# Layer 0 attention: row maxima taken apart into steps and laid between projections and between exponentials

## The chip, the cores and the metric

The kernel runs on one core of one Trainium2 chip, as one launch. The metric is the device time in microseconds. Five engines work side by side, each through its own queue in order: TensorE (PE, matrix products and transposes, with its weight loads shown as PEld), VectorE (DVE), ScalarE (ACT), GpSimd (POOL) and SyncE (SP, which issues most DMAs).

## The reference, cut to what matters

The program is a network of four layers on x of 2 x 1024 x 1024 (batch, tokens, features), float32, each layer an attention-like part and a feed-forward part, each followed by x + f(x) and a normalization over the features. The change lies in the first part of layer 0:

```
qk = (x @ Wqk_w.T + Wqk_b).reshape(b, n, H, E, 2)      # H = 8 heads, E = 16
q, k = the two last indices of qk;  v = x @ Wv_w.T + Wv_b
scores = einsum('bhqd,bhkd->bhqk', q, k)
attn = softmax(scores, axis=-1) / sqrt(128)
out = einsum('bhsl,bhlv->bhsv', attn, v)
return out @ Wo_w.T + Wo_b
```

So q, k and v have 128 features together (8 heads of 16), and each of the 1024 queries of a batch attends to all 1024 keys in each head.

## The kernel before, in words

Batch after batch goes through all layers (net_kernel). x lies in SBUF as eight tiles of 128 tokens x 1024 features, and a transposed copy xT as eight blocks of 128 features x 1024 tokens. to_xT(tt) (L113 to L123) makes xT of one tile: eight transposes on TensorE (L119) into two PSUM banks, and one eviction each, by VectorE and ScalarE in turn (evac, L94). PSUM is one pool of eight banks of 128 x 512 float32; every ps() takes one, and it is free again when its last reader is done.

For batch 0 x is loaded at the start. For batch 1 its tiles are loaded at the end of the last layer of batch 0, each after the output tile in the same place has been stored (load_x). Then all eight tiles are transposed, and l0(b) begins.

l0 loads wqkv (three tiles: q, k, v), wo, the row l0_bo, up and down through SP, and adds the row to all eight tiles of x on POOL (add_row, L126, one 128 x 1024 addition each). It then works in halves th of 512 tokens:

- Projections (L241 to L259): for each half and each s of q, k, v, eight matmuls of 128 x 128 by 128 x 512 into one bank (mm, L104), then an eviction with bias on VectorE (st, L248). For q and k, eight DMAs on SP (L252) spread the heads: qT[g][th] and kT[g][th] hold four heads each (g = 0, 1), one head in each 32 partitions: 16 features, and more rows which POOL had set to 0 in qT and to 1 in kT. For v, four transposes (L256) and two copies on VectorE (L259).
- maxima(th) (L261): for each of 16 steps (g, 128 queries, half of the keys), four matmuls with 32 rows each (L270), one head each, give scores in four banks, and VectorE reduces each to its row maximum (L281). TensorE is kept one step ahead: the next step's scores are issued after the second reduction. After both halves of the keys, a small reduction writes the negated maximum into nmax (L285). After all queries of a g, nmax is transposed (L291) and added to qT (L292), into the row that meets the ones of kT. So the scores that attend computes have the maximum taken off already.
- attend(th, extra) (L294): for each of 16 steps (g, 128 keys), four score matmuls in the other orientation, keys in partitions (L304), four exponentials on ScalarE from PSUM into pt (L312), and four output matmuls, each into 32 partitions of the bank po (L322). A column of ones in v gives the sums of the exponentials. Step n issues the exponentials of n + 1, the scores of n + 2, the outputs of n, and then what extra has for n. done(g) (from L329) turns the result back with four transposes (L332) and divides by the sums.

The order at the end of l0 (from L464) is written out by hand, inside manual_schedule: maxima(0), attend(0), maxima(1), attend(1). What stands outside of such a block, as projections, memsets and loads did, is ordered by a planner, which may put a later part's loads and memsets between; so the row l1_bv of the next part (L91) and the mask (L502), which need a buffer that add_row or a projection frees, stand among the DMAs and memsets of layer 0. Into attend(1) go, as extra, the output projection of the first half (project), the normalization and the transposes of the result. The feed-forward part follows.

The rows l0_bo, l1_projb and l1_bv share two buffers; weight tiles (w) share eight. All eight are taken by wqkv, wo, up and down; the first weights of the next part (l1_conv) and the mask come into those of wqkv when these are no longer read.

Of the kernel before, what the change touches and what calls it, by code (L numbers as in the profile page):

```python
# [11 lines left out]
AF = mybir.ActivationFunctionType  # L12
# [5 lines left out]
P = 128  # L18
# [3 lines left out]
NT = S // P  # L22
KD = D // P
HALF = 512
# [3 lines left out]
class Net:  # L28
# [174 lines left out]
    def l0(self, b):  # L203
        nc, i = self.nc, self.i
        wqkv = [self.w(i["l0_wqkv"][j]) for j in range(3)]
        wo = self.w(i["l0_wo"])
        row = self.row("l0_bo")
        for tt in range(NT):
            self.add_row(row, tt)
        up = [self.w(i["l0_up"][j]) for j in range(2)]  # L210
        down = [self.w(i["l0_down"][j]) for j in range(2)]
        xd, yd = [[self.dp.tile([D, HALF], F, name=self.nm(n)) for _ in range(2)] for n in ("xd", "yd")]
        with self.tc.tile_pool(name=self.nm("l0a"), bufs=1) as lp, self.tc.tile_pool(name=self.nm("l0b"), bufs=2) as tp:
            bias = self.param(lp, "l0_bqkv", [P, 3])
            idx = self.param(lp, "l0_perm", [P, KD], I)

            def piece(name):
                return lp.tile([P, HALF], F, tag="t", bufs=24, name=self.nm(name))
# [6 lines left out]
            qT, kT = [[[piece(n) for _ in range(2)] for _ in range(2)] for n in ("qT", "kT")]  # L225

            v = [piece("v").rearrange("p (a h e) -> p a h e", a=2, h=8) for _ in range(4)]
            ao = lp.tile([P, NT, P], F, name=self.nm("ao"))
            for g in range(2):
                for th in range(2):  # L230
                    nc.gpsimd.memset(qT[g][th], 0.0)
                    nc.gpsimd.memset(kT[g][th], 1.0)
            for t in v:
                nc.gpsimd.memset(t, 0.0)
                nc.gpsimd.memset(t[:, :, :, 16:17], 1.0)
# [2 lines left out]
            for t in nmax:  # L238
                nc.gpsimd.memset(t, 0.0)

            for th in range(2):  # L241
                for s, dst in ((0, qT), (1, kT), (2, v)):
                    p = self.ps()
                    self.mm(
                        p, [(wqkv[s][:, k * P : (k + 1) * P], self.xcols(k, th * HALF, HALF)) for k in range(KD)]
                    )
                    st = piece("st")
                    nc.vector.tensor_scalar(st, p, bias[:, s : s + 1], None, ALU.add)  # L248
                    if s < 2:
                        for h in range(8):  # L250
                            j = h % 4
                            nc.sync.dma_start(dst[h // 4][th][32 * j : 32 * j + 16, :], st[16 * h : 16 * h + 16, :])  # L252
                        continue
                    p = self.ps()
                    for q in range(4):
                        nc.tensor.transpose(p[:, q * P : (q + 1) * P], st[:, q * P : (q + 1) * P], self.ident)  # L256
                    pv = p.rearrange("p (q h e) -> p q h e", q=4, e=16)
                    for a in range(2):
                        nc.vector.tensor_copy(v[2 * th + a][:, :, :, 0:16], pv[:, 2 * a : 2 * a + 2])  # L259

            def maxima(th):  # L261

                steps = [(g, qt, kh) for g in range(2) for qt in range(4) for kh in range(2)]

                def scores(g, qt, kh):

                    pss = [self.ps() for _ in range(4)]
                    for j in range(4):
                        r = slice(32 * j, 32 * j + 32)
                        nc.tensor.matmul(  # L270
                            pss[j], qT[g][th][r, qt * P : (qt + 1) * P], kT[g][kh][r, :], start=True, stop=True
                        )
                    return pss

                todo = scores(*steps[0])
                for n, (g, qt, kh) in enumerate(steps):
                    pss = todo
                    if kh == 0:
                        mx = self.small([P, 4, 2], "l0mx")
                    for j in range(4):  # L280
                        nc.vector.tensor_reduce(mx[:, j, kh : kh + 1], pss[j], AX.X, ALU.max)  # L281
                        if j == 1 and n + 1 < len(steps):
                            todo = scores(*steps[n + 1])
                    if kh:
                        nc.vector.tensor_reduce(  # L285
                            nmax[g][:, qt].rearrange("p (j e) -> p j e", e=32)[:, :, 16], mx, AX.X, ALU.max, negate=True
                        )
                    if qt == 3 and kh:
                        p = self.ps()
                        for q in range(4):  # L290
                            nc.tensor.transpose(p[:, q * P : (q + 1) * P], nmax[g][:, q], self.ident)  # L291
                        nc.vector.tensor_tensor(qT[g][th], qT[g][th], p, ALU.add)  # L292

            def attend(th, extra):  # L294

# [67 lines left out]
            def project(tt):  # L363
                p = self.ps()
                nc.tensor.transpose(p[:, :P], ao[:, tt, :], self.ident)
                aoT = tp.tile([P, P], F, tag="aoT", name=self.nm("aoT"))
                nc.vector.tensor_copy(aoT, p[:, :P])
                for nh in range(2):
                    p = self.ps()
                    nc.tensor.matmul(p, aoT, wo[:, nh * HALF : (nh + 1) * HALF], start=True, stop=True)  # L370
                    self.add_x(tt, nh, p)
                self.ln_stats(tt)

            def store(th):
                for k in range(KD):
                    nc.sync.dma_start(xd[th][k * P : (k + 1) * P, :], self.xcols(k, th * HALF, HALF))
# [3 lines left out]
            def gather(th, n=KD):  # L380
                for j in range(len(ts[th]), len(ts[th]) + n):
                    t = piece("t")
                    nc.gpsimd.indirect_dma_start(
                        out=t, out_offset=None, in_=xd[th][:],
                        in_offset=bass.IndirectOffsetOnAxis(ap=idx[:, j : j + 1], axis=0),
                    )
                    ts[th].append(t)
# [55 lines left out]
            def back(th):  # L443
                ys = [piece("y") for _ in range(KD)]
                for k, t in enumerate(ys):
                    nc.sync.dma_start(t, yd[th][k * P : (k + 1) * P, :])
                return ys

            def line(th, first, n):


                t4 = [4 * th + q for q in range(4)]
                e = {}
                for tt, m in zip(t4, n[:4]):
                    e.setdefault(m, []).append(lambda tt=tt: first(tt))
                e.setdefault(n[4], []).append(lambda: self.ln_roots(t4))
                for tt, m in zip(t4, n[5:]):
                    e.setdefault(m, []).append(lambda tt=tt: (self.ln_scale(tt), self.to_xT(tt)))
                return e

            def at(extra, n, f):
                extra.setdefault(n, []).append(f)

            got = {}  # L464
            with self.tc.manual_schedule():
                self.table()
                maxima(0)
                attend(0, {})
                maxima(1)
                e = line(0, project, (0, 1, 3, 4, 5, 6, 7, 8, 9))  # L470
                at(e, 9, lambda: store(0))
                at(e, 9, lambda: gather(0))
                attend(1, e)
                project(4)
                project(5)
                e = line(1, project, (-1, -1, 0, 0, 1, 1, 2, 2, 3))
                del e[-1]
                at(e, 3, lambda: store(1))
                for n in (5, 6):
                    at(e, n, lambda: gather(1, 2))  # L480
                at(e, 7, lambda: gather(1, 4))
                blocks(0, e)
                ys = back(0)
                e = line(0, lambda tt: self.add_y(tt, ys), (2, 3, 3, 4, 5, 6, 6, 7, 7))
                blocks(1, e)
# [1279 lines left out]
def net_kernel(tc, ins, out):  # L1765
    with ExitStack() as ctx:
        net = Net(ctx, tc, ins, out)
        for tt in range(NT):
            net.load_x(0, tt)
        for b in range(B):  # L1770
            for tt in range(NT):
                net.to_xT(tt)
            with tc.tile_pool(name=net.nm("l1o"), bufs=1) as op:
                w = net.l1_ffn(b, *net.l1_attn(b, net.l0(b), op))
            net.late(b, net.l2_attn(b, w))
# [100 lines left out]
```

## Time and profile before

| what | us |
|---|---|
| median of 3 runs | 5486.4 |
| these runs | 5469.3 to 5487.4 |
| the profiled execution | 5484.1 |
| its span, first to last instruction | 5482.4 |
| TensorE busy in the span | 5094.7 (93%) |
| VectorE busy | 3189.5 (58%) |
| POOL busy | 2025.3 (37%) |
| ScalarE busy | 1934.7 (35%) |

The mean granted TensorE clock is 0.952 of full speed. In the profile a row such as "61.32 19.24 PE L270 MATMUL ps<-kT,qT 32*128 32x512 f32 x64 [0.40 <-DMA kT<-st]" gives start, length, engine, line, operation, output and inputs, tile in the array, how many instructions are drawn together, and in brackets how long the engine had been idle before and what ended that. One float32 matmul of the program is two matmul rows. The ends of matmuls are modelled, so long rows of TensorE may hold waiting. The stages of layer 0 in batch 0 are: transposes to 15 us, projections from 15.3 to 59.8, maxima(0) to 102.8, attend(0) to 140.9, maxima(1) to 183.7; in batch 1: transposes from 2736.6, projections from 2756.6 to 2803.0, maxima(0) to 2846.0, attend(0) to 2883.8, maxima(1) to 2926.6.

### The profile page before, as it was taken

How to read it: one execution, taken by the hardware profiler on the slowest of the kernel's cores; microseconds unless marked ns; L12 is line 12 of the kernel's file. 1: busy time of each engine (PE TensorE's matmuls, PEld its weight loads, DVE VectorE, ACT ScalarE, POOL GpSimd, SP SyncE). 2: the span in 40 equal slices, each digit the busy share in tenths (PEclk: the TensorE clock that was granted, in tenths of full speed). 3: DMA queues.
4: the chain of work that ended last, by engine and by line, in shares of the span. 5: the costliest groups of instructions: out<-in, count | busy, mean ns of one | idle time of the engine just before them, and what ended most of it. 6: DMA issues, size and time to landing. Idle time of an engine off the chain costs nothing.

```text
span 5482.4 us, 52348 instructions
## 1 busy us (share of the span) xinstructions
PE 5094.7 (93%) x17864; PEld 2576.6 (47%) x17864; DVE 3189.5 (58%) x4380; ACT 1934.7 (35%) x3913; POOL 2025.3 (37%) x1195
## 2 busy tenths in 40 slices
PE   9879988999999999998988899889999999999989
PEld 4346745444444444453444476554444444444533
DVE  3553255269989995324345412542799899953143
ACT  2321232267766541011023312323677665410110
POOL 1013120077778883101010120200777788821010
PEclk8889999999999999999987999999999999999999
DMA  2145211277787995110211432112877979950100
GB/s 89 37 144 180 97 54 36 95 219 212 208 246 223 270 256 178 43 65 8 83 33 33 140 115 93 49 44 98 230 213 204 245 220 262 257 173 36 62 8 31
DMA packets 263134, 725.30 MB, mean 132 GB/s; under 512 B 37424, under 2 KB 54448, under 8 KB 262868
## 3 DMA queue, kind: packets, MB, share of 16 engines
q1 hardware_dynamic: 256596, 700.97, 42.8%
q0 software_dynamic: 6272, 20.98, 1.1%
q8 instruction: 143, 2.34, 0.2%
q14 instruction: 123, 1.01, 0.1%
HBM read 616.70 MB, written 103.02 MB: 131 GB/s over the span
## 4 chain that ended last, share of the span: by engine, by line
PE 52%; DVE 10%; ACT 2%; DMA 1%; issue 1%; POOL 0%; SPq 0%; DVEq 0%; ACTq 0%; POOLq 0%
PE ps L104 22%; PE ps L1191 4%; PE ps L1516 4%; PE ps L1301 4%; DVE h L1198 3%; PE ps L1340 3%; PE ps L1220 3%; PE ps L567 3%; PE ps L119 2%; DVE h L1209 2%; DVE x L175 1%; PE ps L1254 1%; ACT ps L1193 1%; DVE st L152 1%; PE ps L270 1%
## 5 line engine op out<-in xcount | busy, mean ns | idle before, releaser
L1183 POOL TENSOR_TENSOR h<-h,br 128x1024 f32<-128x1024 f32 x512 | 1204.2, 2374 | 24.4 <-DMA h<-dxd 13.3
L1193 ACT ACTIVATE ps<-ps,l_Alog 128x512 f32<-128x512 f32 x1024 | 669.1, 660 | 687.4 <-PE ps L1191 680.6
L1191 PE MATMUL ps<-hi,rep 128*128 128x512 f32 x1024 | 757.5, 740 | 21.0 <-DVE h L1198 14.9
L1198 DVE TENSOR_TENSOR_SCAN h<-ps,h 128x512 f32<-128x512 f32 x512 | 606.3, 1212 | 159.1 <-ACT ps L1193 102.6
L1198 DVE TENSOR_TENSOR_SCAN h<-ps,hst,h 128x512 f32<-128x512 f32 x512 | 642.1, 1298 | 14.5 <-ACT ps L1193 14.3
L1209 DVE TENSOR_TENSOR h<-h,ps 128x1024 f32<-128x1024 f32 x512 | 619.5, 1211 | 0.0
L104 PE MATMUL ps<-w,xT 128*128 128x512 f32 (+1 forms) x1280 | 518.3, 562 | 0.0
L1301 PE MATMUL ps<-xT,w 128*128 128x512 f32 x1024 | 513.7, 605 | 0.0
L1220 PE MATMUL ps<-h,sel 128*32 128x512 f32 x2048 | 409.4, 616 | 73.7 <-DVE h L1209 73.4
L1502 POOL TENSOR_TENSOR x<-x,row 128x1024 f32<-128x1024 f32 x48 | 112.9, 2352 | 883.6 <-PE ps L119 883.6
L141 DVE TENSOR_TENSOR x<-x,ps 128x512 f32<-128x512 f32 x192 | 129.3, 686 | 528.4 <-PE ps L104 377.6
L104 PE MATMUL ps<-xT,w 128*128 128x512 f32 x960 | 421.2, 595 | 0.2 <-DMA w<-l_wqkv 0.2
L1191 PE MATMUL ps<-lo,rep 128*128 128x512 f32 x1024 | 408.6, 399 | 0.0
L104 PEld LDWEIGHTS ps<-w,xT 128*128 128x128 f32 x1280 | 247.3, 195 | 255.5 <-issue 248.5
L1191 PEld LDWEIGHTS ps<-hi,rep 128*128 128x128 f32 x1024 | 195.4, 191 | 346.2 <-issue 239.4
L119 PE MATMUL ps<-ident,x 128*128 128x128 f32 x1024 | 162.8, 314 | 151.9 <-DVE x L175 134.6
L104 PEld LDWEIGHTS ps<-xT,w 128*128 128x128 f32 x960 | 182.1, 190 | 230.1 <-issue 227.7
L1191 PEld LDWEIGHTS ps<-lo,rep 128*128 128x128 f32 x1024 | 195.9, 191 | 200.6 <-issue 195.4
L1149 POOL TENSOR_TENSOR e<-e,one 128x512 f32<-128x512 f32 x64 | 81.5, 1273 | 557.9 <-ACT one L1146 364.4
L166 ACT ACTIVATE rs<-mv 128x1 f32<-128x1 f32 (+2 forms) x88 | 17.9, 203 | 760.1 <-DVE mv L160 759.9
L1301 PEld LDWEIGHTS ps<-xT,w 128*128 128x128 f32 x1024 | 188.3, 191 | 174.3 <-issue 149.7
L1340 PE MATMUL ps<-w,w 128*128 128x512 f32 x512 | 269.0, 607 | 0.0
(272 smaller groups left out, 7628.0 us busy)
## 6 DMA issues: line engine op xcount, KB each, us to landing
h<-dxd SPq DMA_DIRECT2D x512, 512.0 KB
w<-l_in SPq DMA_DIRECT2D x128, 512.0 KB
w<-l_out SPq DMA_DIRECT2D x96, 512.0 KB
w<-l_conv SPq DMA_DIRECT2D x54, 512.0 KB
w<-cvd SPq DMA_DIRECT2D x36, 512.0 KB
w<-l_fw SPq DMA_DIRECT2D x32, 512.0 KB
xcd<-xo SPq DMA_DIRECT2D x64, 256.0 KB
szd<-zo SPq DMA_DIRECT2D x64, 256.0 KB
```

What stands on the lines that cost most here:

```text
L104: self.nc.tensor.matmul(out, lhsT, rhs, start=j == 0, stop=j == n - 1)
L119: nc.tensor.transpose(p[:, j * P : (j + 1) * P], self.x[:, tt, k * P : (k + 1) * P], self.ident)
L567: nc.tensor.matmul(w["p", j // 2][:, 256 * (j % 2) : 256 * (j % 2) + 256], w["w"][j][:, k * P : (k + 1) * P], moving(th, j, k), start=k == ...
L1183: nc.gpsimd.tensor_tensor(hs[k], hs[k], norms[of(k)[0]][1].unsqueeze(1).to_broadcast([P, 2, HALF]), ALU.mult)
L1191: nc.tensor.matmul(dA[k, m], rep[:, 8 * jj + 4 * m + q, :], hl[u, c][n], start=n == 0, stop=n == 1)
L1193: nc.scalar.activation(dA[k, m], dA[k, m], AF.Exp, scale=A[:, g : g + 1])
L1198: nc.vector.tensor_tensor_scan(hs[k][:, m, :], dA.pop((k, m)), hs[k][:, m, :], hst[:, g : g + 1] if u else 0.0, ALU.mult, ALU.add)
L1209: nc.vector.tensor_tensor(hs[k], hs[k], norms[of(k)[0]][3].unsqueeze(1).to_broadcast([P, 2, HALF]), ALU.mult)
L1220: nc.tensor.matmul(py[u, c][32 * j : 32 * j + 32, :], self.sel[:, q, :], hs[k - 1 + j // 2][:, j % 2, :], start=False, stop=q == 3,)
L1301: nc.tensor.matmul(p, w["w"][:, k * P : (k + 1) * P], self.xcols(k, u * HALF, HALF), start=k == 0, stop=k == KD - 1)
L1340: nc.tensor.matmul(p, y[:, cc, t * P : (t + 1) * P], wt[:, cc * HALF : (cc + 1) * HALF], start=c2 == 0 and cc == 0, stop=last,)
L1516: nc.tensor.matmul(acc[tt], y[:, cc * HALF + tt * P : cc * HALF + (tt + 1) * P], w[:, cc * HALF : (cc + 1) * HALF], start=c == 0, stop=c = ...
```

## The change

Three things are done.

1. The projections become a generator qkv(s, th, scalar), which issues two of its eight matmul blocks and then hands back control. With scalar set, the eviction is on ScalarE in place of VectorE. The copies of v are always on ScalarE. They all stand inside the block ordered by hand. First come k and q of half 0, whole. Then the transposes of tiles 4 to 7, which net_kernel no longer does. Then k of half 1. The rest, q of half 1 and v of both halves, makes 14 pieces (4, 5 and 5), one of which follows each step of maxima(0).
2. maxima hands back control after each step too. maxima(1) is no stage of its own any more: one of its 16 steps follows each of the 16 steps of attend(0).
3. add_row for tiles 0 to 3 stands between the memsets of qT and kT and those of v; for tiles 4 to 7 it comes after maxima(0).

```diff
-        for tt in range(NT):
-            self.add_row(row, tt)
...
+            for tt in range(4):
+                self.add_row(row, tt)
             for t in v:
...
-            for th in range(2):
-                for s, dst in ((0, qT), (1, kT), (2, v)):
-                    p = self.ps()
-                    self.mm(
-                        p, [(wqkv[s][:, k * P : (k + 1) * P], self.xcols(k, th * HALF, HALF)) for k in range(KD)]
+            def qkv(s, th, scalar):
+                p = self.ps()
+                for k in range(KD):
+                    nc.tensor.matmul(
+                        p, wqkv[s][:, k * P : (k + 1) * P], self.xcols(k, th * HALF, HALF), start=k == 0, stop=k == KD - 1
                     )
-                    st = piece("st")
+                    if k % 2 and k < KD - 1:
+                        yield
+                st = piece("st")
+                if scalar:
+                    nc.scalar.activation(st, p, AF.Identity, bias=bias[:, s : s + 1])
+                else:
                     nc.vector.tensor_scalar(st, p, bias[:, s : s + 1], None, ALU.add)
+                if s < 2:
+                    dst = (qT, kT)[s]
+                    for h in range(8):
+                        j = h % 4
+                        nc.sync.dma_start(dst[h // 4][th][32 * j : 32 * j + 16, :], st[16 * h : 16 * h + 16, :])
+                    yield
+                    return
+                yield
+                p = self.ps()
+                for q in range(4):
+                    nc.tensor.transpose(p[:, q * P : (q + 1) * P], st[:, q * P : (q + 1) * P], self.ident)
+                pv = p.rearrange("p (q h e) -> p q h e", q=4, e=16)
+                for a in range(2):
+                    nc.scalar.copy(v[2 * th + a][:, :, :, 0:16], pv[:, 2 * a : 2 * a + 2])
+                yield
...
                         nc.vector.tensor_tensor(qT[g][th], qT[g][th], p, ALU.add)
+                    yield
...
                 self.table()
-                maxima(0)
-                attend(0, {})
-                maxima(1)
+                for s in (1, 0):
+                    for _ in qkv(s, 0, False):
+                        pass
+                for tt in range(4, NT):
+                    self.to_xT(tt)
+                for _ in qkv(1, 1, False):
+                    pass
+                side = [f for s, th in ((0, 1), (2, 0), (2, 1)) for f in [qkv(s, th, True)] for _ in range(5 if s else 4)]
+                for n, _ in enumerate(maxima(0)):
+                    for f in side[:1]:
+                        next(f)
+                        del side[0]
+                for f in side:
+                    next(f)
+                for tt in range(4, NT):
+                    self.add_row(row, tt)
+                m = maxima(1)
+                attend(0, {n: [lambda: next(m)] for n in range(16)})
                 e = line(0, project, (0, 1, 3, 4, 5, 6, 7, 8, 9))
...
         for b in range(B):
-            for tt in range(NT):
+            for tt in range(4):
                 net.to_xT(tt)
```

More of the change, by code (lines that the diff above doesn't have):

```diff
@@ L239, in l0 @@
                 nc.gpsimd.memset(t, 0.0)
-            for th in range(2):
-                for s, dst in ((0, qT), (1, kT), (2, v)):
-                    p = self.ps()
-                    self.mm(
-                        p, [(wqkv[s][:, k * P : (k + 1) * P], self.xcols(k, th * HALF, HALF)) for k in range(KD)]
-                    )
-                    st = piece("st")
-                    nc.vector.tensor_scalar(st, p, bias[:, s : s + 1], None, ALU.add)
[L249 to L259, printed above, removed]
+            def qkv(s, th, scalar):
[3 more added lines that the diff above has]
+                        p, wqkv[s][:, k * P : (k + 1) * P], self.xcols(k, th * HALF, HALF), start=k == 0, stop=k == KD - 1
+                    )
+                    if k % 2 and k < KD - 1:
[4 more added lines that the diff above has]
+                else:
+                    nc.vector.tensor_scalar(st, p, bias[:, s : s + 1], None, ALU.add)
+                if s < 2:
[13 more added lines that the diff above has]
+                yield
```

## The prediction, made before the changed kernel was run

> **What bounds the kernel now.** I read the page first (chain of waits, slices), then the busy times in windows cut at the stages of layer 0, then the timeline of single engines inside them. The page's chain is carried by TensorE and little else:
>
> ```profile
> PE 52%; DVE 10%; ACT 2%; DMA 1%; issue 1%; POOL 0%; SPq 0%; DVEq 0%; ACTq 0%; POOLq 0%
> ```
>
> Busy shares over the whole span say little about this change: it touches about 170 us of the first half (15 to 184 us, batch 0) and 190 us of the second (2737 to 2927 us, batch 1). The windows of batch 0 decide there; columns are PE, PEld, DVE, ACT, POOL busy, then granted clock, DMA share, GB/s:
>
> ```profile
> 15.00:37.00 22.00, 20.97 (x50) 8.98 (x48) 2.67 (x4) 0.59 (x1) 16.51 (x8) 1.00 0.53 205
> 37.00:60.00 23.00, 22.04 (x60) 10.00 (x64) 3.05 (x6) 0.00 (x0) 2.47 (x3) 1.00 0.33 82
> 60.00:104.00 44.00, 41.33 (x144) 27.53 (x144) 41.75 (x76) 0.00 (x0) 0.00 (x0) 0.59 0.06 18
> 104.00:141.00 37.00, 36.22 (x268) 10.14 (x264) 2.40 (x6) 32.83 (x64) 0.00 (x0) 0.94 0.00 1
> 141.00:184.00 43.00, 40.73 (x140) 25.52 (x144) 41.46 (x77) 0.00 (x0) 0.00 (x0) 0.64 0.00 0
> ```
>
> Each stage has another master. Projections (15 to 60): TensorE alone. maxima(0) and maxima(1) (60 to 104, 141 to 184): VectorE, 41.5 of 43 us, eight reductions in 4.88 us. TensorE is shown busy too, but its rows are long because they wait for PSUM banks and run at 0.59 of the clock. attend(0) (104 to 141): ScalarE, 2.06 us for four exponentials. So stages with different masters stand in a row, and the change lays them beside each other. Batch 1 adds a hole: its last transposes wait for tile 7 of x, behind which all projections stand.
>
> ```profile
> 2736.64 6.28 PE L119 MATMUL ps<-ident,x 128*128 128x128 f32 x56
> 2754.86 1.94 PE L119 MATMUL ps<-ident,x 128*128 128x128 f32 x8 [11.95 <-DMA x<-x]
> 2756.59 22.79 PE L104 MATMUL ps<-xT,w 128*128 128x512 f32 x48
> ```
>
> **Front part, batch 0.** One projection is 16 matmul rows of 0.43 us, 6.86 us. The first wqkv tile landed at 15.1 us; DMA runs at about 415 GB/s there, so the second one, with which k now starts, lands 1.3 us later: start 16.4. k and q of half 0: 13.7, to 30.1. Transposes of tiles 4 to 7: 4 x 1.06 = 4.2 plus 0.7 for the last eviction, to 35.0. k of half 1: 6.9, to 41.9. Before 42 nothing else is late: l_bqkv landed at 27.3, and 16 DMAs of kT and qT at 0.62 us each on SP end near 38, landing 1.9 us later. Then comes a new wait. Scores of step 1 need kT of half 1, which the DMAs bring:
>
> ```profile
> 57.30 4.94 SPq L252 DMA_DIRECT2D kT<-st  x8
> 61.32 19.24 PE L270 MATMUL ps<-kT,qT 32*128 32x512 f32 x64 [0.40 <-DMA kT<-st]
> ```
>
> The fourth DMA is issued 1.9 us after the first and lands 1.9 us later; with the eviction (0.75) and signals, step 1 begins 5.4 us after k ends, at 47.3. Behind that matmul all side projections are queued on TensorE, so only step 0's reductions are covered.
>
> From there maxima(0) has 15 steps. A step's four scores take 1.07 us at full clock, a side piece of two k-blocks 4 x 0.43 = 1.72. So 12 of the 14 pieces make a step of about 2.85 us, above VectorE's 2.49; the other two (four transposes, 0.66) leave it at VectorE's 2.5. 15 x 1.12 + 12 x 1.76 + 2 x 0.8 = 39.5 on TensorE, 2 for the transposes of nmax in the middle, 4.5 for the last reductions, transposes and addition (before: 99.2 to 103.6): 46, to 93.3. The projection holds one bank, so a step's fourth score waits for the first reduction of the step before (0.75 us after its scores), which ends within the side piece: no cost. The three evictions and four copies given to ScalarE, 0.6 us each, are free: it is idle from 16 to 105 us; without that cover they would cost 4 us. An Identity needs no table load (none stands at L573 or L661). On POOL, add_row(0..3) now stands ahead of the memsets of v and nmax: row l_bo lands at 20.5, so these end near 33, and nmax is first written after 50. Moved add_row(4..7), 9.3 us from about 35, has nobody waiting until project(4); beside such adds a small VectorE operation took 1.80 us in place of 0.16 (2741.24), which here falls into the wait for kT.
>
> Here a rule speaks against the change. The Trainium skill, "TensorE: Matmul & The Clock Gate", Part 1, says that an idle window of about 3.4 us puts the array to half clock and a busy one brings it back. The 4 us idle time before step 1 (k's last matmul and one score group aside) is such a window. The trace agrees on the size: after the 11.95 us hole the clock was 0.50 until about 2761, and the first matmuls took 0.86 in place of 0.43 us. By the rule 3.4 us at half clock cost 1.7; if the gate misses the gap, 0. I take 1.5: attend(0) starts at 94.8, against 102.8: **8.0 us won**.
>
> **Front part, batch 1.** Transposes of tiles 0 to 3: 2736.6 to 2741.3. Weights are there (DMA is busy to 2742.7 with all eight, wqkv first). k, q: to 2755.0, which covers the wait for tile 7; it landed at 2754.8, and hardly later now, since only half of POOL's add_row still runs beside VectorE's last normalization. Transposes: to 2760.0; k of half 1: 2766.9; wait 5.4; 46 + 1.5: 2819.8, against 2846.0: **26.2 us won**, 12 of it the hole and about 3 the half clock behind it.
>
> **attend(0) with maxima(1).** Before: 102.8 to 183.7 and 2846.0 to 2926.6, 80.9 and 80.6 us. Now each of 16 iterations has three matmul groups: scores for attend (1.07), outputs (1.00), scores for maxima (1.07), which follow each other so at full clock:
>
> ```profile
> 112.91 1.06 PE L322 MATMUL ps<-pt,v 128*32 128x512 f32 x8
> 113.91 1.14 PE L304 MATMUL ps<-qT,kT 32*128 32x512 f32 x8
> 114.98 1.06 PE L322 MATMUL ps<-pt,v 128*32 128x512 f32 x8
> ```
>
> The same skill's "TensorEngine Tiling (Array Packing)", Key Properties, says that a change of the tiling mode drains TensorE. Here groups of 32 rows and 32 columns alternate and a group still takes 1.0 to 1.07, where two matmuls of 0.43 in a row need 0.86: the drain is within 0.2 us. So its price is in my groups already; counted again it would be 0.4 an iteration, 6 us a stage.
>
> The lower bound is thus 3.14 us. But PSUM has eight banks: one for the outputs, four with scores for maxima, four for attend. One is missing, so the fourth score matmul of attend waits for the first reduction of the scores just made. Nothing in the trace has both streams; the nearest row has attend with transposes that take two banks:
>
> ```profile
> 214.44 1.09 PE L119 MATMUL ps<-ident,x 128*128 128x128 f32 x8
> 215.47 2.37 PE L304 MATMUL ps<-qT,kT 32*128 32x512 f32 x8
> 217.76 1.07 PE L322 MATMUL ps<-pt,v 128*32 128x512 f32 x8
> ```
>
> There the score group took 2.37, half of it waiting for a bank, and the iteration 4.32. With a reduction (0.68) as releaser in place of a copy and an exponential (1.1), I get 1.07 + 0.75 + 1.0 + 1.0 = 3.85. Below 3.14 nothing can go; the upper end is 5, if two reductions must be waited for. Sum: 14 x 3.85 = 53.9; two last iterations without scores of attend 5; first groups 3.2; in the middle and at the end all reductions must end before nmax is transposed, 3.3 and 4; done(1) 1.5; half clock at its start 2: **72.9 us, 8 won per batch**. attend(1) and all behind it are unchanged and start earlier, TensorE being the chain; l_conv loads still come long before their use.
>
> **Sum.** 8.0 + 26.2 + 2 x 8 = 50 us. The profiled run took 5484.1 (span 5482.4), so 5434; the median of the three runs is 2.3 higher: 5436, 0.9% faster. About 0.5% (27 us) is what a measurement of this kernel can tell from no change; its three runs spread over 18 us.
>
> **Rivals.**
> (1) Waits for banks or SP eat more. If an iteration takes 4.8, each stage is 13 longer and 24 remain: 5462. The same comes from SP: row l_bv (L91) waits for the last add_row; before, it stood ahead of the q DMAs (issued 39.00, then 39.42). If it still does, kT comes up to 11 us later per batch: 5458. Against: add_row(4..7) now follows the transposes, so it should be queued after kT and qT of half 0.
> (2) The clock stays at half in the merged stage, and the kernel gets slower. For: maxima had TensorE "busy" and yet 0.50 for 30 us. A score group cold takes 2.0 (three in 6.06 from 102.79); an iteration 3 x 1.9 + 0.75 = 6.5; the stage about 114, 33 longer than now. 66 lost against 34 won in front: 5518. It decides above 5.6 us per iteration. Against: in maxima the array moves data for 0.86 of 2.49 us (35%), here 2.58 of 3.85 (67%); in 262 to 269 us PE was busy 2.1 of 3.4 (62%) and kept 1.00, and attend(0) woke it within 5 us.
> (3) It goes better: reductions never hold a bank back (3.3 per iteration), no half clock: 16 + 7 more, 5413.
> (4) It doesn't do what it says: the order stays stage by stage (the side pieces all wait at the end of the queue) and only the hole is filled: about 5472, or, with lost overlap elsewhere, no change.
>
> **Chances.** As worked 0.50 (5421 to 5451), rival 1 0.20, rival 2 0.09, rival 3 0.11, rival 4 0.10. The range 5408 to 5474 takes in the first, second and fourth of these cases. Faster by over 0.5% (below 5459): 0.50 + 0.11 + half of rival 1, 0.71. Slower by over 0.5%: most of rival 2, 0.08. Between: 0.21.
>
> **What would show it.** Right: no idle PE row of 12 us at 2743; kT's DMA named before the second score group with about 4 us; steps of 2.9 us in maxima(0) at clock 1.00; iterations of 3.7 to 4 in attend(0), its scores released by VectorE. attend(1) starts near 168 and 2877 (2893 less batch 0's 16). Wrong: granted clock 0.5 through the merged stage, iterations above 5, or SP standing at row l_bv with kT behind it.

## The result, and the profile after

The changed kernel takes 5437.4 us in the median of five runs (5424.9 to 5445.2). The kernel before, in five runs (the three shown above and two more), takes 5477.2 (5469.3 to 5487.4). The ratio is 0.9924, with a 95% interval of 0.9902 to 0.9945: faster by 30 to 54 us. The forecast was 5436, 50 us less than the median of 5486.4 shown then. The profiled execution took 5434.3 us, its span 5432.5, 49.9 less than before.

Windows of batch 0, cut at the stages of the changed kernel (PE, PEld, DVE, ACT, POOL busy, granted clock, DMA share, GB/s):

```profile
16.60:32.70 16.10, 16.07 (x33) 6.97 (x34) 0.75 (x1) 0.00 (x0) 9.28 (x4) 0.86 0.69 253
32.70:43.80 11.10, 10.75 (x53) 6.39 (x51) 3.38 (x5) 2.37 (x4) 9.27 (x4) 1.00 0.12 26
43.80:54.50 10.70, 8.05 (x21) 2.70 (x20) 6.07 (x10) 0.00 (x0) 0.50 (x2) 0.72 0.28 74
54.50:93.80 39.30, 39.30 (x172) 14.16 (x171) 33.33 (x59) 3.35 (x7) 0.00 (x0) 0.99 0.12 34
109.60:134.40 24.80, 24.80 (x157) 7.29 (x153) 15.38 (x27) 12.39 (x24) 0.00 (x0) 1.00 0.00 1
```

VectorE's stages at clock 0.59 and 0.64 are gone. The fourth row is maxima(0) beside the projections: TensorE at clock 0.99 and VectorE busy 33 of 39 us. The fifth is a piece of attend(0) beside maxima(1): VectorE and ScalarE are busy for 15 and 12 of 25 us. TensorE looks full, but its rows there hold waiting (see the merged stage below). Two rows are colder than the rest, the first (0.86) and the third (0.72).

In the timeline of TensorE the hole in batch 1 has closed; the transposes, eight per tile, now stand in two groups of four tiles, with k and q between:

```profile
2731.19 3.66 PE L119 MATMUL ps<-ident,x 128*128 128x128 f32 x32
2735.96 13.98 PE L246 MATMUL ps<-xT,w 128*128 128x512 f32 x32 [1.12 <-ACT xT L99]
2749.78 3.66 PE L119 MATMUL ps<-ident,x 128*128 128x128 f32 x32
2753.78 7.14 PE L246 MATMUL ps<-xT,w 128*128 128x512 f32 x16 [0.35 <-DVE xT L97]
```

Read from these timelines, layer 0 splits so (us; "front" runs from the first transpose to the first scores of attend(0), "merged" from there to the first scores of attend(1)):

| stage | before | after | won | forecast |
|---|---|---|---|---|
| front, batch 0 | 97.8 | 91.9 | 5.9 | 8.0 |
| front, batch 1 | 109.4 | 82.6 | 26.8 | 26.2 |
| merged, batch 0 | 80.9 | 74.3 | 6.6 | 8.0 |
| merged, batch 1 | 80.6 | 74.3 | 6.3 | 8.0 |

That is 45.6 of the 49.9 us. The same matmul, counted in order, starts 12.4 us earlier at attend(1) of batch 0, about 15.5 earlier from 400 to 1500 us, only 5.5 at the transposes of batch 1, 38.5 at its attend(1), 49.9 from 5050 us on. So outside of layer 0 the lead over the kernel before moves both ways, down by 10 us (1500 to 2737 us) and up by 14 (from 36.2 at 4200 us).

### The profile page after: what moved, and what is told of

The parts are those of the page before. It is cut to its first block, busy times and chain, and to the rows that moved or that the text cites. A ratio compares the mean times of both kernels' runs of the same rounds, so it can differ in the third digit from the quotient of the medians.

```text
span 5432.5 us, 52392 instructions
## 1 busy us (share of the span) xinstructions
PE 5048.7 (93%) x17864; PEld 2513.1 (46%) x17864; DVE 3184.1 (59%) x4366; ACT 1942.7 (36%) x3927; POOL 2027.0 (37%) x1195
## 5 line engine op out<-in xcount | busy, mean ns | idle before, releaser
L1328 PE MATMUL ps<-xT,w 128*128 128x512 f32 x1024 | 513.6, 605 | 0.0
L104 PE MATMUL ps<-xT,w 128*128 128x512 f32 x768 | 336.1, 593 | 0.0
L1328 PEld LDWEIGHTS ps<-xT,w 128*128 128x128 f32 x1024 | 188.1, 190 | 173.3 <-issue 148.0
L1281 PE MATMUL ps<-xT,w 128*128 128x512 f32 x512 | 266.1, 605 | 2.0 <-DVE h L1225 1.9
```

Source lines behind the costliest of these rows:

```text
L104: self.nc.tensor.matmul(out, lhsT, rhs, start=j == 0, stop=j == n - 1)
L1281: nc.tensor.matmul(p, w["w"][:, k * P : (k + 1) * P], self.xcols(k, u0, HALF), start=k == 0, stop=k == KD - 1)
L1328: nc.tensor.matmul(p, w["w"][:, k * P : (k + 1) * P], self.xcols(k, u * HALF, HALF), start=k == 0, stop=k == KD - 1)
```

## Experiments

Ten runs follow, each timed beside runs of the kernel before on the same chip. Times of different groups are compared by their ratios to that kernel. The text set off in each was written before it ran. Stage times are those of one profile of each kernel.

**1. The changed kernel again** (no edit).

> The changed kernel itself, once more. Theory (the gain is made in layer 0 alone and the rest of the program only wanders by itself from run to run): attention of layer 0 takes the same to within 1 us (attend(1) begins near 171.3 us, and 156.9 us after the first transposes of batch 1), while the lead or lag in the long scan stage (about 1500 to 2400 us and 4200 to 5050 us) differs by several us from the first profile. Rival (the change itself moves something behind layer 0, by DMAs that start earlier): the loss of 10 us between 1500 and 2370 us and the gain of 14 us between 4200 and 5050 us come again at the same places. Time near 5437 us by both.

Measured: 5436.5 us, ratio 0.9914 (0.9897 to 0.9932). Batch 1: front 82.6, merged 74.3, again. Batch 0: front 92.4, merged 75.5; so attend(1) begins at 173.2, and the 1 us that the theory allowed is missed there by 0.9. The longer merged stage ran at clock 0.93, where the first profile has 0.96. Against the first profile of the same program, this one lies 7.3 us behind at 1430 us, 0.5 behind at 2440, 6.8 ahead at 3850 and 0.9 behind at 4790. So the long stages wander by that much without any change. Against before, the scan stages again first lose and then gain, but 3 to 4 us in place of 10 and 14. The wander explains most; that a few us of it are the change's is not excluded.

**2. Front alone.**

```diff
-                m = maxima(1)
-                attend(0, {n: [lambda: next(m)] for n in range(16)})
+                attend(0, {})
+                for _ in maxima(1):
+                    pass
```

> Side pieces and the order of projections as changed, but maxima(1) is a stage of its own again behind attend(0). Theory (stages win separately: front 5.8 us in batch 0 and 26.8 us in batch 1, merged stage 6.6 and 6.3 us by the profile of after): 33 us are won against before, 5444 us beside 5477. Rival (without the side-by-side attend(0), the half clock of maxima(1) and a cold start of attend(1) cost more than counted, or the merged stage brings nothing): 5450 or more, or the same as the changed kernel, 5437.

Measured: 5455.6 us, ratio 0.9954 (0.9936 to 0.9971): 25 us won, interval 16 to 35. The median lies nearer to the rival. Its stages don't: front 90.9 and 82.6 us, attend(0) with maxima(1) behind it 80.9 and 80.6, exactly as before, which makes 33.7 won in layer 0; the profiled execution is 33.8 us shorter than before. The start of attend(1) is no colder than in the changed kernel (clock 0.86 and 0.84 in its first 13 us, there 0.87). So the stages agree with the theory, and its 33 us lie inside the interval of the times.

**3. Only the transposes moved behind projections.**

```diff
-                for _ in qkv(1, 1, False):
-                    pass
-                side = [f for s, th in ((0, 1), (2, 0), (2, 1)) for f in [qkv(s, th, True)] for _ in range(5 if s else 4)]
-                for n, _ in enumerate(maxima(0)):
-                    for f in side[:1]:
-                        next(f)
-                        del side[0]
-                for f in side:
-                    next(f)
+                for s, th in ((1, 1), (0, 1), (2, 0), (2, 1)):
+                    for _ in qkv(s, th, False):
+                        pass
+                for _ in maxima(0):
+                    pass
```

with the edit of run 2 as well. The order of add_row and the copies of v on ScalarE stay as in the changed kernel, here and in run 4.

> Only the order of transposes and projections: k and q of half 0, transposes of tiles 4 to 7, then the other four projections whole, then maxima(0), attend(0), maxima(1) each alone. Theory (the wait for tile 7 is covered in batch 1, about 12 us; in batch 0 four transposed tiles no longer lie in the shadow of the first loads, and the array stands idle before k, about 8 us lost): about 4 us won in all, 5473. Rival (most of the 27 us won in front of batch 1 is the hole and the half clock behind it, side pieces bring little): 15 us or more won, 5462 or less.

Measured: 5477.9 us beside 5480.7, ratio 0.9992 (0.9981 to 1.0003). The front takes 105.1 us in batch 0, 7.3 longer than before, and 96.3 in batch 1, 13.1 shorter. So this part alone is worth little: batch 0 pays for what batch 1 wins. The rival, that the hole carries the front's gain, falls for the sum, though the order makes 13.1 of the 26.8 us won in batch 1. The rest of the front comes with the side pieces: between this run and run 2 the front falls from 105.1 to 90.9 us and from 96.3 to 82.6, 14 us in each batch. How much of that is the move of three evictions to ScalarE (4 us by the prediction) was not run apart.

**4. Merged stage alone.**

```diff
-                for s in (1, 0):
-                    for _ in qkv(s, 0, False):
-                        pass
                 for tt in range(4, NT):
                     self.to_xT(tt)
...
+                for th in range(2):
+                    for s in range(3):
+                        for _ in qkv(s, th, False):
+                            pass
+                for _ in maxima(0):
+                    pass
```

> All transposes, then the six projections whole, maxima(0) alone, as before; only maxima(1) goes in steps beside attend(0). Theory (merged stage 74.3 us in place of 80.8, the bank that is missing sets 3.95 us per iteration): 13 us won, 5464. Rival (the merged stage is carried by the clock or by what the front left behind, so that alone it brings nothing): 5474 or more.

Measured: 5469.1 us, ratio 0.9975 (0.9966 to 0.9985), 14 us by the ratio. Front 98.3 and 109.2 as before, so the moved add_row and the copies of v on ScalarE bring nothing by themselves. Merged 74.3 and 73.1. Runs 2 and 4 together give the gain of the changed kernel (25 and 14 against 42), within their intervals.

**5. One PSUM bank fewer in the merged stage.**

```diff
+                hold = self.ps()
+                nc.tensor.transpose(hold[:, :P], self.ident, self.ident)
                 m = maxima(1)
                 attend(0, {n: [lambda: next(m)] for n in range(16)})
+                nc.vector.tensor_copy(self.small([P, 1], "hold"), hold[:, :1])
```

> The changed kernel with one PSUM bank held from the start of attend(0) to its end (written by one transpose, read by one small copy behind the stage), so the merged stage has seven. Theory (iterations are set by the bank that is missing: with eight, the fourth score matmul of attend waits for the first reduction; with seven the third waits for the first and the fourth for the second, 0.60 us later): 4.55 us per iteration in place of 3.95, stage 74.3 to 83, all in all about 17 us slower than the changed kernel, 5454. Rival (iterations are set by TensorE's own work and its changes of tiling mode, or by the order of its queue): 3.95 stays, 5437 to 5440.

Measured: 5459.7 us, ratio 0.9957 (0.9942 to 0.9971), 18 us slower than the changed kernel by the ratios (24 by that of run 1). One iteration in the timeline of TensorE:

```profile
2869.06 2.66 PE L316 MATMUL ps<-qT,kT 32*128 32x512 f32 x8
2871.66 1.06 PE L334 MATMUL ps<-pt,v 128*32 128x512 f32 x8
2872.65 1.14 PE L281 MATMUL ps<-kT,qT 32*128 32x512 f32 x8
2873.61 2.66 PE L316 MATMUL ps<-qT,kT 32*128 32x512 f32 x8
```

From 2869.06 to 2873.61 are 4.55 us, as expected. The row that grew is attend's scores: 2.66, where the changed kernel has 2.06 (below). Their weight loads (PEld, two for each matmul) show the waits one by one. In the changed kernel only the last matmul of the four waits for VectorE:

```profile
115.46 0.29 PEld L316 LDWEIGHTS ps<-qT,kT 32*128 32x128 f32 x2 [0.74 <-DVE l0mx L292]
```

With seven banks the third and the fourth do:

```profile
2870.00 0.29 PEld L316 LDWEIGHTS ps<-qT,kT 32*128 32x128 f32 x2 [0.75 <-DVE l0mx L292]
2870.60 0.29 PEld L316 LDWEIGHTS ps<-qT,kT 32*128 32x128 f32 x2 [0.30 <-DVE l0mx L292]
```

The stage became 86.7 and 87.8 us, not 83: with the longer waits the clock fell to half for longer (0.89 over the stage, where the changed kernel has 0.96).

**6. Maxima of three heads in four.** In maxima(1) `range(4 - th)` takes the place of `range(4)` for banks, matmuls and reductions; heads 3 and 7 of half 1 get neither queries (left at zero) nor maxima, and nmax is set to zero once between.

> The changed kernel with maxima(1) over three heads of four: heads 3 and 7 of the second half get no maxima (their queries of that half are left at zero, so that the exponentials stay finite), and each step uses three banks, three matmuls, three reductions. Theory (the missing bank): 1 + 4 + 3 banks fit into eight, nobody waits for a reduction just begun, an iteration is three groups back to back: 3.0 to 3.3 us, stage near 63, 23 us faster than the changed kernel, 5414. Rival (TensorE's own work with its mode changes takes 3.9): three matmuls of a group run at once, so the group costs the same, 3.9 stays, and only the reductions at the ends shrink by 1 to 2 us a stage, 5434.

Measured: 5414.4 us, ratio 0.9882 (0.9866 to 0.9899). Two iterations in the timeline:

```profile
2817.48 1.06 PE L336 MATMUL ps<-pt,v 128*32 128x512 f32 x8
2818.47 1.13 PE L283 MATMUL ps<-kT,qT 32*128 32x512 f32 x6
2819.34 1.12 PE L318 MATMUL ps<-qT,kT 32*128 32x512 f32 x8
2820.40 1.06 PE L336 MATMUL ps<-pt,v 128*32 128x512 f32 x8
2821.39 1.30 PE L283 MATMUL ps<-kT,qT 32*128 32x512 f32 x6
2822.36 1.37 PE L318 MATMUL ps<-qT,kT 32*128 32x512 f32 x8
```

2.92 and 3.26 us in turn, stage 60.2 us. A group of six rows for maxima takes 0.87 to 0.97 us until the next, one of eight 0.96, so TensorE's work hardly fell. The wait did: from 2811 to 2830 us the scores of attend wait for no reduction any more, only now and then for ScalarE (us in total, times, longest):

```profile
PEld ps L318 <- ACT pt L326: 0.5, 2, 0.2
```

This kernel also leaves out a quarter of VectorE's reductions; run 5, which leaves them all in, moves the iteration the other way by the bank alone. Runs 5 and 6 together settle it: the bank, and not TensorE's work or its changes of mode, makes 3.95 us of 3.1.

**7. Three side pieces ahead of maxima(0).**

```diff
+                for _ in range(3):
+                    next(side.pop(0))
                 for n, _ in enumerate(maxima(0)):
```

> The changed kernel with the first three side pieces (q of half 1) issued ahead of maxima(0), so that TensorE works while kT of half 1 is on its way; the last three steps of maxima(0) then have no piece beside them. Theory (the idle time before step 1 and the half clock that follows it cost some 7 us per batch; the steps without a piece run at VectorE's 2.5 us): granted clock 1.00 through this place, attend(0) begins 5 us earlier in each batch, 5427. Rival (that time is not on the path: VectorE with 64 reductions sets the stage, or the pieces only shift): within 1 us per batch, 5436.

Measured: 5434.3 us, ratio 0.9915 (0.9899 to 0.9932): as the changed kernel. Both sides were half right. The front took 89.6 and 80.1 us, 2.3 and 2.5 less, but the merged stage 76.4 in both batches, 2.1 more. Where the gain of the front went is seen in the windows of batch 1 (from 2762.8, maxima(0) with pieces, its last steps without, the start of the merged stage):

```profile
2762.80:2795.50 32.70, 32.70 (x148) 11.63 (x147) 28.91 (x51) 2.71 (x5) 0.00 (x0) 1.00 0.12 32
2795.50:2808.10 12.60, 9.79 (x41) 4.54 (x40) 12.01 (x23) 0.65 (x2) 0.00 (x0) 0.80 0.08 30
2808.10:2823.00 14.90, 14.90 (x69) 6.33 (x72) 5.73 (x10) 8.31 (x16) 0.00 (x0) 0.73 0.00 1
```

The same place in the changed kernel, from the last reductions on:

```profile
2808.80:2813.80 5.00, 2.22 (x16) 1.00 (x15) 4.49 (x9) 0.65 (x2) 0.00 (x0) 0.94 0.19 72
2813.80:2826.40 12.60, 12.60 (x66) 5.31 (x65) 5.72 (x10) 8.31 (x16) 0.00 (x0) 0.89 0.00 1
```

With the steps without a piece the clock fell (0.80), and the merged stage began at 0.73 in place of 0.89.

**8. Step of maxima(1) ahead of the outputs.** In attend, the functions of `extra` are called before `outputs(n)`, for this stage alone.

> The changed kernel with the step of maxima(1) ahead of the four output matmuls in each iteration of attend(0), so that the outputs run on TensorE while the first reduction frees the bank for attend's scores. Theory (bank waits): the wait moves to the scores for maxima, which then need the first exponential of the scores just made (0.52 us instead of 0.60, and a little of VectorE's last releases): 3.8 us per iteration and 1 to 2 us less at the turn of nmax, 5 us faster in all, 5432. Rival (TensorE's own order and mode changes): outputs between the two score groups saved a mode change; now two groups of 32 rows stand together and one change falls away, also a little faster; or slower by over 5 us, if exponentials now start late. Tells little between theory and rival, but it is a candidate for a better order.

Measured: 5426.7 us, ratio 0.9898 (0.9885 to 0.9912). Merged stage 69.8 us, 4.5 less:

```profile
2833.86 1.06 PE L334 MATMUL ps<-pt,v 128*32 128x512 f32 x8
2834.85 1.14 PE L316 MATMUL ps<-qT,kT 32*128 32x512 f32 x8
2835.82 1.97 PE L281 MATMUL ps<-kT,qT 32*128 32x512 f32 x8
2837.71 1.07 PE L334 MATMUL ps<-pt,v 128*32 128x512 f32 x8
```

```profile
PEld ps L281 <- ACT pt L324: 10.1, 23, 0.8
```

The iteration takes 3.85 us (3.80 expected), and the wait stands where it was expected, in the scores for maxima (1.97), their weight loads released by ScalarE. 14 x 0.10 is 1.4 of the 4.5 us. Most of the rest is at the turn of nmax, where three iterations take 14.4 us in place of 17.5; the clock is 1.00 there and 0.87 in the changed kernel, so a part of it is the clock. The rival's premise does not hold: in both kernels an iteration has one group of outputs and two groups of scores side by side, so no change of mode falls away.

**9. Pieces ahead, the others spread.** As run 7, with pieces after steps 0, 1, 3, 4, 6, 7, 9, 10, 12, and two after 14.

> As the run that issued three side pieces ahead of maxima(0), but with the eleven others spread over its 16 steps, so that steps without a piece stand in between and the last two pieces stand in the wait for the last reductions. Theory (that run won 2.4 us per batch in front, and gave it back since four steps without pieces at the end let the clock fall to half, so that the merged stage began cold: 76.4 in place of 74.3): clock near 1.00 up to the merged stage, which takes 74.3 or 1 to 2 less; 3 to 5 us won per batch, 5429. Rival (maxima(0) with fewer pieces is VectorE's, whatever the order, and the start of the merged stage is cold because of the last reductions anyway): as that run, 5434.

Measured: 5422.6 us, ratio 0.9895 (0.9876 to 0.9915). Front 88.0 and 78.4 us, 3.9 and 4.2 less than in the changed kernel; merged 74.5. All of maxima(0) ran at clock 1.00, in batch 1 for instance:

```profile
2755.80:2799.30 43.50, 42.72 (x181) 17.12 (x180) 40.53 (x73) 2.97 (x6) 0.00 (x0) 1.00 0.10 26
2820.00:2870.00 50.00, 49.92 (x279) 15.22 (x272) 31.35 (x57) 20.97 (x40) 0.00 (x0) 0.93 0.00 1
```

The gain that run 7 gave back is kept, by the stages; the interval of the whole time overlaps with that of the changed kernel. A merged stage below 74 did not come of the warm start: it fell to half clock once later (second row).

**10. Runs 8 and 9 together.**

> The same spreading, and the step of maxima(1) ahead of the outputs in attend(0), which alone made the merged stage 69.8 us. Theory (the two do not touch each other: one is the front, the other the banks): 3 to 5 us per batch less than 5427, 5419. Rival (as for the other): 5427.

Measured: 5418.3 us, ratio 0.9888 (0.9868 to 0.9908), the lowest median of the kernels that compute everything: front 88.5 and 78.4 as in run 9, merged 68.9 and 69.1 us as in run 8. So the two gains add up in the stages. The whole times do not tell this run from runs 8 and 9: the intervals overlap.

## Why the prediction was right

**What bounds the stages** was right: by runs 2 and 4 the stages gain separately, and stages with different masters did fit beside each other.

**Front, batch 0** was mis-sized by 2.1 us. The term "k and q of half 0: 13.7" measured 16.0. I charged a half clock to the wait for kT and not to the first wait, though the sum itself left the array idle from the last early transpose to the second wqkv tile:

```profile
11.60:16.60 5.00, 0.00 (x0) 0.00 (x0) 0.29 (x1) 0.59 (x1) 0.00 (x0) 0.77 1.02 410
16.60:21.60 5.00, 4.97 (x7) 2.18 (x8) 0.00 (x0) 0.00 (x0) 1.13 (x1) 0.55 1.03 387
```

Five us without a matmul, then seven rows in five us at 0.55. Start (16.63 for 16.4) and the last k (7.1 for 6.9) were right; the transposes took 4.0 us for 4.9. In batch 1, where the weights were there and the clock stood at 1.00, k and q took 13.8 us, and the front came out at 82.6 us for 83.2.

**The new wait for kT** was there. SP stood at row l_bv until add_row(7) ended (43.09), then kT came:

```profile
43.09 0.34 SPq L91 DMA_DIRECT2D row<-l_bv  x1
43.47 1.38 SPq L1466 DMA_DIRECT2D idx<-l_perm  x3
44.95 4.93 SPq L260 DMA_DIRECT2D kT<-st  x8
```

```profile
47.54 3.36 PE L281 MATMUL ps<-kT,qT 32*128 32x512 f32 x8 [2.65 <-DMA kT<-st]
50.83 3.78 PE L246 MATMUL ps<-xT,w 128*128 128x512 f32 x4
54.54 1.47 PE L281 MATMUL ps<-kT,qT 32*128 32x512 f32 x8
57.85 1.14 PE L281 MATMUL ps<-kT,qT 32*128 32x512 f32 x8
```

Row l_bv stood behind kT and qT of half 0, as argued against rival 1, and cost nothing: the eviction of k ended at 44.60, and kT was issued at 44.95, behind the index loads, so they delayed it by 0.35 us at most. (I had named SP at row l_bv with kT behind it as a sign of being wrong; it was seen, without the cost.) Step 1 began before all four heads had landed, by the look of its weight loads, which come 0.6 to 0.7 us apart as kT's DMAs do; so the wait ahead is 2.65 us and the rest lies inside the 3.36; and the side piece took 3.78 in place of 1.92. From k's end to the scores of step 2 the forecast was 5.4 + 1.1 + 1.8 + 1.5 = 9.8 us; it was 10.7, and 10.4 in batch 1. So the half clock cost 2.1 to 2.4 rather than 1.5, if the wait itself was sized right. The step that failed here is its length: I had taken 3.4 us at half clock, and it was 6.8, behind the first wait as well as here:

```profile
14.30:21.10 6.80, 4.47 (x6) 1.92 (x7) 0.00 (x0) 0.00 (x0) 0.63 (x1) 0.50 1.03 393
48.40:55.20 6.80, 6.80 (x14) 2.31 (x15) 2.83 (x5) 0.00 (x0) 0.00 (x0) 0.50 0.09 19
```

That this place is on the path, runs 7 and 9 show. A steady step of maxima(0) took 2.99 us (57.85, 60.84, 63.83 and so on) for 2.85.

**Merged stage.** The mechanism was right in each link. The timeline in batch 0, and what the weight loads of attend's scores waited for over the stage (us in total, times, longest):

```profile
113.56 1.14 PE L281 MATMUL ps<-kT,qT 32*128 32x512 f32 x8
114.52 2.06 PE L316 MATMUL ps<-qT,kT 32*128 32x512 f32 x8
116.51 1.07 PE L334 MATMUL ps<-pt,v 128*32 128x512 f32 x8
117.51 1.14 PE L281 MATMUL ps<-kT,qT 32*128 32x512 f32 x8
```

```profile
PEld ps L316 <- DVE l0mx L292: 9.8, 18, 0.7
```

3.95 us per iteration for 3.85, attend's scores stretched to 2.06, their weight loads released by VectorE. 14 x 0.10 is as much as the whole difference between 74.3 and 72.9, but that is luck, since other terms cancel. In batch 0 the 14 iterations and the turn of nmax (102.27 to 163.75) took 61.5 us where 53.9 + 3.3 stood: the first iteration took 6.3 us, and the turn 5.7 more than three iterations at 3.95. The end took 7.5 where 5 + 4 + 1.5 stood. (The sum of 3.85 was itself a slip: its four terms make 3.82.) The price taken for the change of tiling mode, none beyond the groups, holds: with three heads per step three groups, with two changes of mode, followed each other in 2.92 us.

**Rivals.** The clock (2) stayed at 1.00 in the steady part, as the window from 109.6 to 134.4 shows; it did fall at the start and around the turn of nmax (0.87 from 134.4 to 147.8). One of my arguments against it was misread: attend(0) of the kernel before came to full clock 5.7 us after its start (108.5), not within 5. Waits for SP (1) were not met. Of fewer waits for banks (3), run 6 shows what it would have brought. That nothing but the hole counts (4) is excluded by run 3.

**Luck.** The profiled span fell by 49.9, the forecast was 50; but 45.6 of it are layer 0's, and the rest can be wander that could have had the other sign: the medians differ by 40, the ratio makes it 42. That 5436 is met to 1.4 us is luck too: the median of five runs of the kernel before is 9.2 us below the one I started from, and the gain is about as much smaller. I also put attend(1) of batch 1 at 2877; it began at 2888.1, since the lead had shrunk to 5.5 us on the way.

## What to carry to other kernels

Where stages with different masters stand in a row, lay one beside the other step by step, and count PSUM banks before engines: 4 + 4 + 1 banks in eight set the iteration here (3.95 us, against 3.1 where one stream needed a bank fewer, and 4.55 where a bank was taken away). Put the work that needs no bank behind the user whose bank comes back later (outputs behind the scores for maxima: 3.85 in place of 3.95 us per iteration). A gap in TensorE's queue cost its length here and then the half clock behind it (2.3 us behind a gap of 5.0), so pieces are best kept for the waits and spread, not used up at once.

## What had not been expected of the hardware

How long TensorE's rows look did not tell the clock. Rows of maxima alone stand back to back in the kernel before, and the clock was 0.50 for 30 us; the merged stage, back to back as well, held 1.00 (109.6 to 134.4 above). The prediction had judged by the share of time in which the array moves data at full clock, an estimate from 0.43 us per matmul row: 35% in maxima alone (0.86 of 2.49 us), 65% in a merged iteration (2.58 of 3.95), 57% with seven banks (2.58 of 4.55). The runs fit it only in part. With seven banks the clock held for some iterations and then fell behind the turn of nmax. And in maxima(1) of the kernel before, whose steps are those of maxima(0), it came back to 1.00 for a while and fell again to 0.50. The first two rows are the kernel before, the others run 5:

```profile
69.00:99.00 30.00, 30.00 (x97) 21.52 (x93) 29.10 (x54) 0.00 (x0) 0.00 (x0) 0.50 0.00 1
166.50:173.00 6.50, 6.50 (x25) 3.14 (x22) 6.46 (x12) 0.00 (x0) 0.00 (x0) 1.00 0.00 0
2868.00:2882.70 14.70, 14.70 (x80) 4.94 (x76) 6.42 (x11) 6.76 (x12) 0.00 (x0) 1.00 0.00 1
2883.30:2901.00 17.70, 17.70 (x57) 5.82 (x58) 8.40 (x16) 4.61 (x8) 0.00 (x0) 0.64 0.00 0
```

So no threshold comes out of these runs; what decides the clock was not tried.
